# One list of TensorE instructions with short conditional blocks in place of nine arms per segment, a second buffer for the exponentials, and the next segment prepared over six steps

## Chip, cores and metric

The kernel runs on one core of one Trainium2 chip (trn2). The metric is the device time of one execution in microseconds. The kernel before ran three times: 446.67, 449.19 and 451.4 us, median 449.19.

The engines are named as in the profile: PE is TensorE (matmuls; PEld is its weight load), DVE is VectorE, ACT is ScalarE, POOL is GpSimd, SP is SyncE, which only issues DMAs. A name with a q (PEq, POOLq) is the sequencer of the engine: branches, register loads, DMA issues.

## What is computed

16384 rows of 256 features belong to 8 segments; the segment ids come unsorted. Rows are placed by id and position into padded segments, attention runs inside each segment, its result goes back to the rows, through a linear layer and a batch normalization over all rows, and is added to the input:

```python
q, k, v = feat @ Wq, feat @ Wk, feat @ Wv             # widths 32, 32, 256
starts = searchsorted(bids, arange(8))
pos = arange(N) - starts[bids]
qp, kp, vp = pad(q), pad(k), pad(v)                   # [8, 3072, .], at [bids, pos]
scores = einsum('bld,bmd->blm', qp, kp)
attn = softmax(where(mask, scores, -1e9))
rp = einsum('blm,bmd->bld', attn, vp)
t = rp[bids, pos] @ Wt
tn = (t - t.mean(0)) / sqrt(t.var(0) + 1e-5) * gamma + beta
out = feat + relu(tn)
```

Since the ids are unsorted, only few rows land inside a segment of 3072 places: with this input the segments 0 to 7 fill 4, 4, 5, 6, 6, 6, 4 and 4 tiles of 128 rows. All other rows read the first or last place of a segment.

## The kernel before

`fast_path` is written as one list of operations. The helpers of `Fast` (`mm` L790, `tr` L795, `act` L800, `copy` L805 and L806, `tt` L809, `ts` L816 and L818, `stt` L829, `recip` L842, `dma` L860, `gather` L865, `put` L875) append an operation to the list of `Program`, which works out from the memory that each one reads and writes which others it has to wait for, and hands each engine its operations in the order of writing. So the order of the work on each engine is the order in which the Python code calls the helpers. Every operation of a helper carries that helper's line in the profile, so groups are told apart by the names of tiles.

The stages:

- *Start.* The ids are loaded; DVE and small matmuls find the segment starts. For segments 0 and 1 the owned rows are counted with a scan into `lm` (L838) and `prefix`, and `make_list` turns this into a list of row numbers: two comparisons into `ge`, matmuls of `ge` with `lm`, and DVE instructions on the result (`lr`, `junk`, `jc`, `idx`); then six indirect DMAs on POOL fetch the rows into `xs`. Six places per segment are always listed and fetched, whatever its length.
- *Segments*, eight times, `e` being the current one and `n` the next. Preparing a segment: `xt_main` and `xt_rest` transpose `xs` on PE and copy it with ACT into `xT`; `project` makes q (DVE, with a copy on ACT of its last 32 partitions) and k (small DVE copies, L806) for the first four tiles (`c=0`) and the last two (`c=1`); `values` makes v times Wt (`vs`, an ACT copy); `scores(e, c, tiles)` multiplies k with q and takes the exponential on ACT into `pa` (queries of tiles 0 to 3, 512 columns per key tile) or `pb` (queries of tiles 4 and 5, 256 columns). `attend(e, u)` multiplies the exponentials with `vs` for query tile `u`; a column of ones in `vs` gives the denominators, DVE takes the reciprocal `rdens` and multiplies into `tk`, and SP stores `tk` into `t_rows` after u = 3 and u = 5.
- *Statistics.* `gather_reads` fetches how often each place is read (`reads_r`, POOL), and `moments` adds tk and its square (`sq`, ACT) times these counts into `acc` (two DVE instructions of L829 per tile).
- *Work items.* Tables over all rows (`everyone`, `tables`, `one_hot`) are cut into pieces of DVE work, and `slot()` writes one piece behind a step.
- *End.* Column sums, scale and shift; then 16 groups of 1024 rows are read (`f`), completed with a one-hot matmul and DVE additions, and stored; the places inside segments are written over by indirect DMAs of POOL (`put`), the fifth and sixth tile of a segment only where it is present (conditional block, L728).

PSUM has eight banks: 0 to 3 for scores, 4 and 5 for attends, 6 and 7 in turn (`nb()`) for all else, the lists, transposes, projections and values. `vs`, `q` and `k` have two buffers, `pa` and `pb` one.

Only the fifth and sixth tile of a segment depend on the data. On PE this is solved with arms: `region(key, arms)` opens a block for which the whole instruction list of a segment is written out for each pair of counts of `e` and `n` (three times three arms), and PE jumps into one with a register loaded from `arm` (L1055 for the loads, L770 for `e.Switch`). ACT and DVE have no arms: they do the work of six tiles in every segment. In a region the code of a step is:

```python
for u in range(FT):
    step(e, u)                  # attend(e, u), one or two moments
    if u == 0 and e + 2 < NB:
        make_list(e + 2, FT)
        gather_reads(e)
    for x in fills[u]: x()      # xt_main(n,0), xt_main(n,1), xt_rest(n), project(n,0)
    if u == 1: scores(e, 1, range(4), 0)
    if u == 2: scores(e, 1, range(4, 6), 0)
    if u == 3: project(n, 1, 1); values(n, 0, 1); scores(n, 0, range(4), None)
    if u == 4: values(n, 1, 1)
    if u == 5: values(n, 2, 1)
    slot(1)
```

The scores of `n` for key tiles 4 and 5 are made inside attend(n, 0). After segment 6 POOL gathers `ecat` from `t_rows` and loads 16 registers (`upto`, `tiles_i`, L1055) before the reads of segment 7.

## Time and profile before

One execution was profiled.

| what | us |
|---|---|
| median of three timed runs | 449.19 |
| span of the profiled execution | 481.6 |
| start, to the first attend | 43.0 |
| segments 0 to 6 | 290.1 |
| segment 7, to the last moment | 27.6 |
| statistics | 11.5 |
| 16 groups | 68.7 |
| last puts and stores | 40.7 |

The profiled execution is 32.4 us longer than the median, so its stages are read for their proportions, and a sum made in it is carried to the timed runs by the ratio 449.19/481.6. The mean clock granted to PE in it is 0.732 of full speed. An f32 matmul appears as two records.

In views by stage, a row holds the bounds, the length, and for each engine the busy time with the count of instructions in brackets; PEclk is the granted clock. In views of waits, a row names an engine, what it was about to do and what it waited for, then the total, the times and the longest. In views of groups, the numbers behind the bar are the total busy time, the mean in ns, and the idle time ahead of the group with what ended it. In the chain and the timeline a row begins with its start and its length.

### The profile page before, as it was taken

Reading aid. Unit: us, or ns where it says so; the run is one execution under the profiler, and the core shown is the slowest. Engines: PE = TensorE matmul, PEld = TensorE weight load, DVE = VectorE, ACT = ScalarE, POOL = GpSimd, SP = SyncE. Lnnn points to the kernel's source line nnn. Section 1 sums busy time; section 2 is a strip of 40 time slices with the busy share of each in tenths; the row PEclk is TensorE's granted clock in tenths of the full one; section 3 lists DMA queues with packets and bytes.
Section 4 is the critical chain, followed back from the end, with each engine's and each line's share of the span. In section 5 each row is a group of like instructions: output and inputs, shape, how many; then the busy total and the mean of one; then the engine's idle time right before and its main releaser. Section 6 shows DMA issues by size and latency. Waiting matters only on the chain.

```text
span 481.6 us, 4068 instructions
## 1 busy us (share of the span) xinstructions
PE 300.9 (62%) x1112; PEld 185.2 (38%) x1112; DVE 278.5 (58%) x775; ACT 116.4 (24%) x240; POOL 160.0 (33%) x159
## 2 busy tenths in 40 slices
PE   1368356452677486959695879797403999966000
PEld 1345233241346363747373657575301343211000
DVE  7664943322978462553554454476545999999400
ACT  0126123102142241223131323366311111100000
POOL 2340001773004522630072017700160034876350
PEclk9998857575878887788887968899855555555555
DMA  8920110120101210210011102102594599999510
GB/s 271 335 68 3 40 36 3 50 62 0 49 27 44 63 38 23 76 60 13 31 53 60 44 2 55 47 25 69 186 406 198 189 398 416 420 416 382 213 61 8
DMA packets 27218, 59.48 MB, mean 124 GB/s; under 512 B 6462, under 2 KB 19856, under 8 KB 23066
## 3 DMA queue, kind: packets, MB, share of 16 engines
q1 hardware_dynamic: 19242, 48.06, 26.7%
q0 software_dynamic: 6288, 10.01, 6.7%
q8 instruction: 35, 0.57, 0.6%
q10 hardware_dynamic: 1632, 0.66, 0.5%
q14 instruction: 21, 0.17, 0.1%
HBM read 26.42 MB, written 28.74 MB: 115 GB/s over the span
## 4 chain that ended last, share of the span: by engine, by line
PE 40%; DVE 28%; issue 12%; another core or an unknown queue 6%; DMA 3%; ACT 3%; POOL 3%; POOLq 2%; SPq 1%; DVEq 0%
PE ps L790 38%; DVE f L809 4%; DVE tk L809 3%; DVE acc L829 3%; PE ps L795 2%; DVE tk L818 2%; POOL out L875 2%; ACT pa L800 2%; DVE k L806 2%; POOLq L1055 2%; DVE junk L816 2%; DMA reads_r<-reads_of,idx 1%; DVE q L818 1%; DMA graw<-in_L_rec_gamma 1%
## 5 line engine op out<-in xcount | busy, mean ns | idle before, releaser
L865 POOL DMA_INDIRECT xs<-in_r_feat,idx x48 | 50.8, 1058 | 184.1 <-DVE junk L816 164.1
L790 PE MATMUL ps<-vs,pa 128*128 128x257 f32 x312 | 92.6, 453 | 28.4 <-DVE tk L818 16.6
L790 PEld LDWEIGHTS ps<-vs,pa 128*128 128x128 f32 x312 | 68.7, 229 | 50.4 <-issue 17.9
L842 DVE RECIPROCAL rdens<-ps 128x1 f32<-128x1 f32 x48 | 8.0, 166 | 98.8 <-PE ps L790 59.9
L790 PE MATMUL ps<-wvt,xT 128*128 128x256 f32 x156 | 46.9, 455 | 28.9 <-DVE k L806 28.9
L875 POOL DMA_INDIRECT out<-tk,idx x39 | 45.4, 1165 | 58.4 <-DVE f L809 33.7
L865 POOL DMA_INDIRECT reads_r<-reads_of,idx x48 | 48.9, 1020 | 23.8 <-issue 23.5
L790 PEld LDWEIGHTS ps<-wvt,xT 128*128 128x128 f32 x156 | 34.8, 230 | 43.9 <-DVE k L806 33.5
L800 ACT ACTIVATE xT<-ps,negx 128x512 f32<-128x512 f32 (+1 forms) x32 | 17.6, 586 | 99.5 <-PE ps L795 62.1
L790 PE MATMUL ps<-y,hot 48*128 48x256 bf16 x128 | 33.4, 409 | 12.3 <-DVE y L806 7.5
L800 ACT ACTIVATE pa<-ps,mask 128x512 f32<-128x512 f32 x48 | 29.6, 689 | 24.7 <-PE ps L790 19.3
L790 PE MATMUL ps<-f,ident 128*128 128x512 f32 x32 | 33.2, 1141 | 0.0
L790 PEld LDWEIGHTS ps<-y,hot 48*128 48x128 bf16 x128 | 12.3, 123 | 51.0 <-issue 24.1
L829 DVE SCALAR_TENSOR_TENSOR acc<-tk,reads_r,acc 128x256 f32<-128x256 f32 x48 | 22.9, 477 | 15.0 <-DMA reads_r<-reads_of,idx 14.6
L809 DVE TENSOR_TENSOR tk<-tk,ss 128x768 f32<-128x768 f32 x32 | 30.5, 955 | 0.6
L809 DVE TENSOR_TENSOR f<-f,ps 128x512 f32<-128x512 f32 x48 | 30.0, 680 | 0.8 <-PE ps L790 0.8
L805 ACT COPY f<-ps 128x512 f32<-128x512 f32 x16 | 9.4, 586 | 66.1 <-PE ps L790 66.1
L829 DVE SCALAR_TENSOR_TENSOR acc<-sq,reads_r,acc 128x256 f32<-128x256 f32 x48 | 23.0, 479 | 3.1 <-ACT sq L800 3.1
L818 DVE TENSOR_SCALAR tk<-ps,rdens 128x256 f32<-128x256 f32 x48 | 23.2, 484 | 1.8
L800 ACT ACTIVATE sq<-tk 128x256 f32<-128x256 f32 x48 | 20.2, 425 | 15.3 <-DVE acc L829 13.5
L790 PE MATMUL ps<-q,k 32*128 32x512 f32 (+2 forms) x124 | 23.1, 654 | 0.0
L795 PE MATMUL ps<-ident,xs 128*128 128x128 f32 x78 | 15.5, 336 | 11.7 <-DVE lr L809 6.8
(229 smaller groups left out, 367.3 us busy)
## 6 DMA issues: line engine op xcount, KB each, us to landing
f<-in_r_feat SPq DMA_DIRECT2D x16, 1024.0 KB, 17.1
out<-f SPq DMA_DIRECT2D x16, 1024.0 KB, 4.8
xs<-zt SPq DMA_DIRECT2D x8, 768.0 KB, 9.9
t_rows<-tk SPq DMA_DIRECT2D x8, 512.0 KB, 3.0
t_rows<-tk SPq DMA_DIRECT2D x8, 256.0 KB, 2.7
eb<-edge_of SPq DMA_DIRECT2D x16, 96.0 KB, 4.5
xs<-in_r_feat,idx POOLq DMA_INDIRECT x48
reads_r<-reads_of,idx POOLq DMA_INDIRECT x48
```

The source lines that it names most:

```text
L790: "PE", lambda e: e.matmul(out, lhsT, rhs, start=start, stop=stop, skip_group_check=True),
L795: return self.op("PE", lambda e: e.transpose(out, in_, ident), [in_, ident], [out], pred=pred)
L800: "ACT", lambda e: e.activation(out, in_, func, bias=bias, scale=scale), [in_, *more], [out]
L805: return self.op("ACT", lambda e: e.copy(out, in_), [in_], [out])
L806: return self.op(eng, lambda e: e.tensor_copy(out, in_), [in_], [out])
L809: return self.op(eng, lambda e: e.tensor_tensor(out, a, b, op), [a, b], [out])
L816: lambda e: e.tensor_scalar(out, a, s1, s2, op0, op1, accum_out=accum)
L818: else e.tensor_scalar(out, a, s1, s2, op0, op1),
L829: else e.scalar_tensor_tensor(out, a, s, b, op0, op1),
L865: lambda e: e.indirect_dma_start(out=out, out_offset=None, in_=table, in_offset=bass.IndirectOffsetOnAxis(ap=ind, axis=0), bounds_check=n ...
L875: lambda e: e.indirect_dma_start(out=table, out_offset=bass.IndirectOffsetOnAxis(ap=ind, axis=0), in_=src, in_offset=None, bounds_check=n ...
L1055: regs[key] = e.value_load(ap, min_val=lo, max_val=hi)
```

## The change

- *PE in one list.* `region`, `arms` and `e.Switch` are gone. An operation written under `with pg.given(e, k)` is done only when the register of segment `e` (0, 1 or 2 for four, five or six tiles) is greater than k; runs of operations with the same condition form one `e.If` block (now at L764). PE has 22 such blocks per segment; ACT has seven and DVE one, which there skip the work of missing tiles. A conditional operation signals nothing itself: whoever waits for it waits for the next unconditional operation on its engine. The three engines load the register once per segment (L686).
- *`pa` has two buffers*, and the scores of `n` for key tiles 4 and 5 are made in segment `e` as well. `pb` keeps one; its exponentials are written as eleven instructions of 128 or 256 columns in place of six of 256.
- *tk and q on ACT.* The multiplication of the attend's result with `rdens` moves from DVE to ACT; q is written by two ACT instructions from PSUM.
- *The next segment over six steps* (diff below). The lists' comparisons (`list_tests`) are made in u = 5 of the segment before the one that uses them, the list halves use score banks 2 and 3. Those of segment 2 are made ahead of the loop.
- *Moments and reads.* The reads of segment e are gathered in segment e + 1; no moments in segments 0 and 1, one or two per step afterwards.
- *Group loads.* All eight buffers of the final stage lie over `pa[0]` and what follows it; the loads of groups 0 to 5 are issued inside segment 7 (groups 0 to 3 in u = 0), those of 6 and 7 after it. Before, all eight came after it.

```diff
-                    if len(arms) == 1:
-                        one(arms[0])
-                    else:
-                        for a in e.Switch(reg["reg"](e), len(arms)):
-                            one(arms[a])
+                    with e.If(self.regs[(eng, o.when[0])] > o.when[1]):
+                        for x in ops[k:end]:
+                            emit(e, x)
...
-    pa = new("pa", [P, FT, QA])
-    pb = new("pb", [P, FT, QB])
+    pa[0] = new("pa0", [P, FT, QA])
...
+    pa[1] = new("pa1", [P, FT, QA])
...
+    def present(e, t):
+        return ExitStack() if t < 4 else pg.given(e, t - 4)
...
-        pg.ts(qe[0:96, lo : lo + n], b[0:96, 0:n], cqk[0:96, :], ALU.add)
-        pg.copy("ACT", qe[96:P, lo : lo + n], qe[0:32, lo : lo + n])
-        for t in range(n // P):
-            g = 32 * t
-            pg.copy("DVE", ke[g : g + 32, c, :], b[96:P, t * P : (t + 1) * P])
+        with present(e, 4 * c):
+            pg.act(qe[0:96, lo : lo + n], b[0:96, 0:n], AF.Identity, bias=cqk[0:96, :])
+            pg.act(qe[96:P, lo : lo + n], b[0:32, 0:n], AF.Identity, bias=cqk[0:32, :])
+            for t in range(n // P):
+                g = 32 * t
+                pg.copy("DVE", ke[g : g + 32, c, :], b[96:P, t * P : (t + 1) * P])
...
-        pg.ts(tk[:, m, :], po[:, 0:D], rdens[:, m : m + 1], ALU.mult)
+        pg.act(tk[:, m, :], po[:, 0:D], AF.Identity, scale=rdens[:, m : m + 1])
...
+            if ahead <= NB and u == 0:
+                first = list_half(ahead, 0, ps_s[2])
+            attend(e, u)
...
+            if ahead <= NB and u == 0:
+                first()
+                if LTs == FT:
+                    second = list_half(ahead, 1, ps_s[3])
+            if e >= 2:
+                for _ in range(2 if u % 2 or len(lag) > 12 else 1):
+                    if lag and lag[0][0] < (e if u > 1 else e - 1):
+                        moments(*lag.pop(0))
+            if e >= 1 or u >= 1:
+                slot(2 if e == 0 else 1)
+            attended(e, u)
...
             if u == 1:
-                scores(e, 1, range(4), 0)
...
+                gather_reads(e - 1) if e else None
+            if n < NB:
+                if u == 0:
+                    xt_main(n, 0)
+                    xt_main(n, 1)
+                if u == 1:
+                    xt_rest(n)
+                if u == 2:
+                    scores(e, 1, None)
+                    project(n, 0)
+                if u == 3:
+                    project(n, 1)
+                    scores(n, 0, range(4))
+                if u == 4:
+                    values(n, 0)
+                    scores(n, 0, range(4, 6))
+                if u == 5:
+                    values(n, 2)
+                    values(n, 1)
+                    if e + 3 <= NB:
+                        list_tests(e + 3, FT if e + 3 < NB else LT)
+            else:
...
+                if u == 1:
+                    gather_reads(e)
+                if u == 0:
+                    for g in range(4):
+                        group_in(g)
```

How the instructions move, at three places. In the rows, psN is the PSUM bank, `ge` and `lm` belong to the lists, `w4` to the projection, `wvt` to the values; "waits at_X" is a semaphore of engine X.

PE, in segment 1, arm of six and six tiles, from the projection of segment 2 to its values, before:

```order
L790 MATMUL ps6<-xT_55,w4_78 128x512 x2
L790 MATMUL ps7<-xT_55,w4_78 128x256 [waits at_ACT]
L790 MATMUL ps7<-xT_55,w4_78 128x256
L790 MATMUL ps6<-wvt_79,xT_55 128x256 [waits at_DVE]
L790 MATMUL ps6<-wvt_79,xT_55 128x256 x3
L790 MATMUL ps0<-q0_56,k0_57 128x512
L790 MATMUL ps1<-q0_56,k0_57 128x512
L790 MATMUL ps2<-q0_56,k0_57 128x512
L790 MATMUL ps3<-q0_56,k0_57 128x512 [waits at_ACT]
L790 MATMUL ps4<-vs1_58,pb_53 128x257 x6
```

and now, in segment 0, whose steps are the same:

```order
L799 MATMUL ps7<-xT_54,w4_79 128x512
L799 MATMUL ps5<-vs0_53,pa0_52 128x257 [waits at_ACT]
L799 MATMUL ps5<-vs0_53,pa0_52 128x257 x2
L764 COMPARE_AND_BRANCH
L799 MATMUL ps5<-vs0_53,pa0_52 128x257
L764 UNCONDITIONAL_BRANCH
...
L799 MATMUL ps0<-q1_63,k1_64 128x512 [waits at_ACT,at_DVE]
L799 MATMUL ps1<-q1_63,k1_64 128x512 [waits at_DVE]
L799 MATMUL ps2<-q1_63,k1_64 128x512 [waits at_DVE]
L799 MATMUL ps3<-q1_63,k1_64 128x512 [waits at_ACT,at_DVE]
...
L799 MATMUL ps7<-wvt_80,xT_54 128x256 x4
```

An attend stands between the projection and the scores; the values, which waited for DVE straight after the projection, come behind the scores and wait for nothing.

PE, at the start of segment 1, the arm of six and six tiles before:

```order
L770 BRANCH_PREFETCH_HINT
L790 MATMUL ps4<-vs1_58,pa_52 128x257
L790 MATMUL ps0<-q1_59,k1_60 128x512
L790 MATMUL ps1<-q1_59,k1_60 128x512
L790 MATMUL ps4<-vs1_58,pa_52 128x257 x2
L790 MATMUL ps4<-vs1_58,pa_52 128x257 [waits at_ACT] x2
L790 MATMUL ps4<-vs1_58,pa_52 128x257
L790 MATMUL ps7<-lm_61,ge_62 128x131 [waits at_DVE] x2
```

and now:

```order
L686 TENSOR_LOAD tiles_i_128
L686 ISA x2
L799 MATMUL ps2<-lm_57,ge_58 128x131 [waits at_DVE] x2
L799 MATMUL ps2<-lm_57,ge_58 128x131 x4
L799 MATMUL ps4<-vs1_66,pa1_65 128x257 x2
L799 MATMUL ps4<-vs1_66,pa1_65 128x257 [waits at_ACT]
L764 COMPARE_AND_BRANCH
L799 MATMUL ps4<-vs1_66,pa1_65 128x257
```

The first list half now stands ahead of the attend, in a score bank, and the scores of key tiles 4 and 5 are no longer inside the attend.

POOL, around the end of segment 6, before:

```order
L865 DMA reads_r<-reads_of,idx 128x1 x12
L865 DMA ecat<-t_rows,eidx 128x256
L1055 TENSOR_LOAD upto
L1055 ISA x2
L1055 TENSOR_LOAD tiles_i
```

and now:

```order
L874 DMA reads_r<-reads_of,idx 128x1 x6
L874 DMA ecat<-t_rows,eidx 128x256
L686 TENSOR_LOAD upto
...
L686 ISA x2
L874 DMA reads_r<-reads_of,idx 128x1 x12
L874 DMA tl<-t_rows,ridl 128x256 x3
```

Six gathers of reads moved from ahead of the `ecat` gather to behind the register loads.

607 lines of the change are left out of this document (286 added, 321 removed).

## Prediction

> **What bounds the kernel now.** I read the busy slices of the page first, then a table by stage, then what TensorE (PE) waits for in the stages that the change touches.
>
> ```profile
> PE 300.9 (62%) x1112; PEld 185.2 (38%) x1112; DVE 278.5 (58%) x775; ACT 116.4 (24%) x240; POOL 160.0 (33%) x159
> ...
> PE 40%; DVE 28%; issue 12%; another core or an unknown queue 6%; DMA 3%; ACT 3%; POOL 3%; POOLq 2%; SPq 1%; DVEq 0%
> ```
>
> No engine is full: PE, the busiest, is busy for 62% of the span, and it leads the chain that ended last with 40%. The shares are means over unlike stages, so the next table cuts the span at the start of each segment's first attend.
>
> ```profile
> core 0: us, PE busy (x) PEld busy (x) DVE busy (x) ACT busy (x) POOL busy (x), PEclk, DMA share, GB/s
> ...
> 43.01:84.15 41.14, 22.45 (x84) 13.69 (x82) 25.01 (x91) 13.57 (x28) 1.14 (x2) 0.74 0.07 24
> 84.15:137.42 53.27, 24.81 (x90) 17.91 (x91) 26.55 (x74) 12.38 (x27) 22.93 (x23) 0.69 0.13 37
> 137.42:181.69 44.27, 32.27 (x137) 22.52 (x137) 29.28 (x100) 12.83 (x27) 16.92 (x16) 0.81 0.16 48
> 181.69:230.49 48.80, 38.91 (x153) 27.42 (x153) 21.56 (x62) 13.10 (x27) 14.62 (x14) 0.79 0.16 48
> 230.49:276.12 45.63, 34.82 (x152) 25.47 (x153) 21.60 (x62) 13.09 (x27) 12.51 (x12) 0.85 0.13 41
> 276.12:315.41 39.29, 33.31 (x137) 23.47 (x137) 18.46 (x61) 12.22 (x26) 19.54 (x18) 0.83 0.12 33
> 315.41:333.06 17.65, 14.71 (x69) 10.63 (x68) 11.24 (x31) 11.64 (x26) 0.00 (x0) 1.00 0.14 47
> 333.06:360.68 27.62, 8.93 (x40) 7.47 (x41) 15.63 (x42) 9.25 (x23) 10.08 (x10) 0.73 0.69 262
> 360.68:372.22 11.54, 4.08 (x5) 1.00 (x5) 6.66 (x21) 2.00 (x3) 0.00 (x0) 0.50 0.55 222
> 372.22:440.92 68.70, 63.85 (x159) 20.20 (x160) 66.75 (x87) 8.79 (x15) 35.21 (x29) 0.50 0.90 364
> ...
> ```
>
> The loop over segments 0 to 6 is the stretch 43.01 to 333.06: 290.05 us, of which PE is busy 22.45 + 24.81 + 32.27 + 38.91 + 34.82 + 33.31 + 14.71 = 201.3 and idle 88.8. DVE (153.7) and ACT (88.8) are well below that, so in the loop PE's own work and its gaps set the pace, but for segments 0 and 1, where DVE is busier than PE. The clock matters as well: multiplying each row's busy time by its PEclk gives 162.6 us of work at full clock, so 38.7 of the 201.3 are the lower clock. The last 148.5 us, where DVE (66.75 of 68.70), the puts and the last DMAs set the end, are the same code in both kernels from the statistics on.
>
> PE's gaps in the loop, by what it waited for:
>
> ```profile
> PE ps L790 <- DVE k L806: 28.9, 7, 6.3
> ...
> PE ps L790 <- DVE tk L818: 16.6, 3, 14.2
> PE ps L790 <- issue: 14.8, 5, 6.2
> ...
> PE ps L790 <- DVE ge L818: 7.6, 4, 1.9
> PE ps L795 <- DVE lr L809: 6.8, 5, 1.5
> ```
>
> Columns: total, times, longest. These five are 74.7 of the 88.8 us.
>
> **Part by part.** *The wait for k (28.9).* `values(n,0)` runs straight after the projection and needs a PSUM bank that DVE still reads for q and k; the scores behind it on PE stand too. The new list puts attend(e,3) between `project(n,0)` and `scores(n,0)`, and attend(e,4) ahead of `values(n,0)`. The cover is real PE work:
>
> ```profile
> 333.06 7.20 PE L790 MATMUL ps<-vs,pa 128*128 128x257 f32 x32 [0.86 <-ACT sq L800]
> 323.25 1.88 PE L790 MATMUL ps<-xT,w 128*128 128x512 f32 x4
> L818 DVE TENSOR_SCALAR q<-ps,cqk 96x512 f32<-96x512 f32 x7 | 5.2, 742 | 7.1 <-PE ps L790 6.4 <-remote 0.7
> L806 DVE COPY k<-ps 32x128 f32<-32x128 f32 x44 | 12.9, 294 | 0.9
> L800 ACT ACTIVATE pa<-ps,mask 128x512 f32<-128x512 f32 x44 | 27.1, 688 | 24.3 <-PE ps L790 18.8 <-issue 5.4
> L800 ACT ACTIVATE pb<-ps,mask 128x256 f32<-128x256 f32 x42 | 17.4, 480 | 7.0 <-PE ps L790 3.9 <-remote 3.1
> L818 DVE TENSOR_SCALAR tk<-ps,rdens 128x256 f32<-128x256 f32 x41 | 19.8, 484 | 1.5
> ```
>
> A record of an attend takes 7.20/32 = 0.225 us, so an attend of a six-tile segment (12 records) covers 2.7 us. Four k copies are 1.18; q moves to ACT as two acts of at most the 688 ns of a 512-wide one. All 28.9 is taken off. What comes back: on ACT q now stands behind the second exponentials, ten of 128 columns and one of 256. From 688 and 480 ns a 128-wide act is an estimated 376, so these are 4.2 us where six of 480 were 2.9; with q (1.4) and a tk (0.42) ACT needs 6.0 us. PE's work between is project(n,0) (1.88), the attend (2.7) and project(n,1) (about 1): 5.6. I charge 1.1 for each of three six-tile segments, 3.4 in all (bounds 0 and the 28.9 itself, if the wait only changes its name).
>
> *The wait for tk (16.6)* is mostly one stall, 14.2 long, seen on the chain too:
>
> ```profile
> 102.48 14.36 another core or an unknown queue
> 112.80 1.00 POOL L865 DMA_INDIRECT reads_r<-reads_of,idx  x1 [0.30 <-issue]
> 206.92 4.61 another core or an unknown queue
> L865 POOL DMA_INDIRECT reads_r<-reads_of,idx x42 | 42.9, 1021 | 12.8 <-issue 12.5 <-DVE lr L809 0.3
> ```
>
> It lies in a run of 24 gathers on POOL that ends at 113.8; in later segments the run is 12 long and the stall 4.61. The new order never queues 24 at once, so I take 16.6 off and put one such 4.6 back. If these stalls came from somewhere else, the 16.6 stays (bounds 0 and 16.6).
>
> *The list waits (7.6 + 6.8).* The comparisons for the list of e+2 are made in the last step of the segment before, and its halves have PSUM banks of their own. The cover is the rest of that segment's DVE queue, 0.4 us each; without it the 14.4 comes back.
>
> *Dispatch (14.8).* Each segment's jump into one of nine arms goes:
>
> ```profile
> L770 PEldq COMPARE_BRANCH  x18: 288/399/5012, 40.4 to 341.0; - x18
> L728 POOLq COMPARE_BRANCH  x16: 34/45/53, 393.8 to 457.0; - x16
> L1055 PEldq TENSOR_LOAD <-arm x9: 296/304/738, 22.7 to 78.9; - x9
> ```
>
> Minimum, median and maximum in ns: the jumps cost up to 5012. In their place PE evaluates 22 conditions per segment and 2 at the end, 178 in all; with segments of 4, 4, 5, 6, 6, 6, 4 and 4 tiles, 101 of them skip. The nearest rows are POOL's short conditional blocks, built the same way, at 45 ns, and PE's own shortest jump at 288. I take 0.1 us, nearer the form than the engine: 17.8 us of sequencer time, of which 44 conditions lie in segments 0 and 1 and 22 in segment 7, where DVE or POOL sets the pace; 112 are left, and I expose 10. Bounds: 178 x 0.034 = 6 all hidden, so 0, and 178 x 0.399 = 71. The loads of the registers, 0.30 us each on three engines per segment, lie beside waits. [...]
>
> *Clock.* The row at 315 shows PE with 14.71 of 17.65 busy at 1.00; the rows with longer gaps show 0.69 to 0.85. With two thirds of the idle time gone the loop is like that row more often. Bounds: 0 and all of the 38.7; I take 18, about half. [...]
>
> *tk to ACT.* 41 x 484 ns leaves DVE (19.8 us) and comes to ACT, which was busy 88.8 of 290; both beside PE.
>
> *Start.* The owners and tests of segment 2 are made before the loop, and the first list half stands ahead of attend(0,0) on PE: some 20 small DVE instructions, 5 us by the 0.29 of a k copy, partly under the projections: +3 (bounds 0 and 6).
>
> *Tail.* The reads of a segment are gathered one segment later, so behind the ecat gather and 16 register loads POOL has twelve, not six:
>
> ```profile
> 337.71 0.30 POOLq L1055
> ...
> 346.25 0.28 POOLq L1055
> ...
> 352.76 5.53 DMA reads_r<-reads_of,idx
> ...
> 360.15 0.49 DVE acc L829
> 360.68 4.09 PE ps L790 x4
> ```
>
> The last reads, at 358.3, release the last moments and these the statistics at 360.68. Six more gathers at (42.9 + 12.8)/42 = 1.33 us are +8.0, and nothing covers them: DVE has only the moments to do (bounds 4, should the register loads start earlier against the segment's end, and 8).
>
> *Group loads.* Four of the final stage's loads are issued in segment 7, on SP ahead of its stores of t rows. Before, all landed before their use at 372.22, so nothing is gained; a late store would cost at most its own
>
> ```profile
> 334.17 2.19 DMA t_rows<-tk
> ```
>
> and I take 0.
>
> **The sum.** -74.7 + 3.4 + 4.6 + 10 - 18 + 3 + 8 = -63.7 us against the profiled span of 481.6: 417.9. The three timed runs have a median of 449.19, 0.933 of that span; by this ratio 417.9 is **390 us**.
>
> **Rivals.** *The wait moves to ACT.* ACT takes its list in order; tk now waits there for a reciprocal that stands behind moments and list work on DVE, and the exponentials, q and xT wait behind tk. If the k wait of 28.9 comes back as a wait for q, the gain is 34.8: 446.8, timed 417. For it: the 6.0 against 5.6 above. Against it: ACT is busy only 13 us in segments of 44 to 49.
>
> *Slower: a hop costs PE what a jump does.* Place: the 101 skipped blocks, 90 of which belong to the segments of four tiles. My sum without the 10 for branches is 73.7; it is eaten when a skip costs 73.7/101 = 0.73 us. The median PE jump is 0.40 and the longest 5.0; at 1.0 the end is 481.6 - 73.7 + 101 = 508.9, timed 475. Against it: POOL's 45 ns.
>
> *Slower: the granted clock stays at a half once PE is dense*, as the row 372.22 to 440.92 shows (63.85 of 68.70 busy at 0.50). Then the 162.6 of work take 325; with start, tail and their 11 us 527.7, timed 492. It decides below a mean of 0.64 (162.6 over the 253 us that are left). Against it: 1.00 in the dense row at 315.41.
>
> *The gaps only move*: attends wait for tk, lists for POOL, and segments 0 and 1 stay with DVE; within 1% of 449.
>
> **How the numbers follow.** Forecast 0.65; wait on ACT 0.22; no change 0.04; dear hops 0.06; half clock 0.03. A measurement of this kernel tells about 1% from no change (446.67 to 451.4). Faster is 0.65 + 0.22 = 0.87, same 0.04, slower 0.09. The range: if every wait goes, hops are free and the clock is full, 481.6 - 74.7 - 38.7 + 11 = 379, timed 354; the ACT rival with 13 us more of branches or waits reaches 430. So 355 to 430.
>
> **What would show it.** Right: in the loop no wait of PE for k over 1 us, no branch record over 1 us, PEclk above 0.85 from segment 2 on, the loop's seven segments in about 218 us, and 35 us instead of 27.62 from the end of segment 6's attends to the last moment. Wrong: waits of PE on q, pa or tk of ACT that sum to over 20 us; branch records of PE with a median above 0.4 us; a clock of 0.5 to 0.7 in rows where PE is busy over 85%; or a loop above 250 us.

## The result and the profile after

The changed kernel takes 424.81 us (median of four runs, 423.68 to 429.4), the kernel before 449.63 (median of four, one of them taken beside it); the ratio is 0.948, 95% interval 0.941 to 0.954. Here and below medians are over all executions and ratios over those within 1.5% of their kernel's fastest, so that a ratio can differ a little from the quotient of two medians, and a single execution of the kernel before at 861 us, beside e1 to e4, is in none. So it is faster by 5%, by 24.8 us where 59 were forecast, and 424.81 lies inside the range of 355 to 430. The profiled execution spans 422.2 us; the forecast of that span was 417.9. The span of before in its profile was 481.6. **The difference of the spans came as forecast, the difference of the times did not.**

The page of the kernel after, busy time by engine:

```profile
PE 287.8 (68%) x1162; PEld 181.8 (43%) x1162; DVE 246.3 (58%) x715; ACT 122.7 (29%) x266; POOL 162.0 (38%) x159
```

The table by stage of the kernel after, cut at each segment's first attend (segments 0 to 6, then segment 7 to the statistics; columns as in the prediction):

```profile
47.81:73.00 25.19, 19.05 (x86) 13.63 (x83) 20.08 (x76) 8.31 (x16) 6.78 (x6) 0.80 0.15 47
73.00:96.95 23.95, 20.59 (x95) 14.35 (x93) 21.54 (x57) 11.34 (x23) 14.00 (x12) 0.93 0.24 73
96.95:130.94 33.99, 27.57 (x139) 20.20 (x137) 22.16 (x78) 16.50 (x38) 12.90 (x12) 0.94 0.18 55
130.94:171.21 40.27, 34.82 (x168) 26.27 (x167) 20.05 (x60) 17.59 (x44) 12.54 (x12) 0.88 0.19 53
171.21:211.73 40.52, 35.47 (x170) 26.48 (x167) 17.71 (x54) 17.01 (x41) 12.14 (x12) 0.87 0.15 45
211.73:243.05 31.32, 29.17 (x146) 22.64 (x143) 13.18 (x52) 13.74 (x34) 12.24 (x12) 0.89 0.14 42
243.05:267.12 24.07, 17.61 (x71) 12.57 (x69) 8.70 (x33) 10.10 (x22) 12.14 (x12) 0.86 0.14 43
267.12:300.93 33.81, 12.11 (x46) 9.17 (x44) 10.98 (x31) 7.75 (x20) 16.47 (x16) 0.65 0.77 289
```

The loop takes 219.3 us (the terms of the sum give 215.4, and about 218 was announced), PE is busy for 184.3 of it and idle for 35.0; the first attend starts at 47.81 in place of 43.01 (forecast +3), and segment 7 to the statistics takes 33.8 us (forecast 35.6). What PE still waits for in the loop (of the rows of PE the five longest):

```profile
PE ps L799 <- ACT q L809: 11.5, 4, 5.2
PE ps L799 <- DVE ge L827: 9.3, 3, 3.1
PE ps L799 <- DVE lm L847: 5.0, 1, 5.0
PE ps L799 <- ACT vs L814: 3.6, 4, 1.2
PE ps L799 <- ACT pa L809: 2.1, 1, 2.1
```

The waits for k, tk and the jumps are gone from this list, and that for `ge`, the comparisons of the lists, is still there. New are those for q, `lm` (which belongs to the lists as well) and pa, and that for vs has grown; three of these four carry the name of ACT. In segment 6, PE's weight loads still wait 5.6 us for k, beside the longest wait for q (see e17).

### The profile page after: what moved, and what is told of

Read it like the earlier page. It is cut to its first block, busy times and chain, and to the rows that moved or that the text cites. A ratio compares the mean times of both kernels' runs of the same rounds, so it can differ in the third digit from the quotient of the medians.

```text
span 422.2 us, 4412 instructions
## 1 busy us (share of the span) xinstructions
PE 287.8 (68%) x1162; PEld 181.8 (43%) x1162; DVE 246.3 (58%) x715; ACT 122.7 (29%) x266; POOL 162.0 (38%) x159
## 5 line engine op out<-in xcount | busy, mean ns | idle before, releaser
L799 PE MATMUL ps<-vs,pa 128*128 128x257 f32 x312 | 80.2, 410 | 0.0
L799 PEld LDWEIGHTS ps<-vs,pa 128*128 128x128 f32 x312 | 62.7, 206 | 13.2 <-issue 3.3
L809 ACT ACTIVATE tk<-ps,rdens 128x256 f32<-128x256 f32 x48 | 22.8, 475 | 128.1 <-DVE rdens L851 128.1
L838 DVE SCALAR_TENSOR_TENSOR acc<-sq,reads_r,acc 128x256 f32<-128x256 f32 x48 | 23.1, 481 | 48.4 <-ACT sq L809 48.4
L799 PE MATMUL ps<-wvt,xT 128*128 128x256 f32 x156 | 41.3, 413 | 5.2 <-ACT vs L814 3.6
L799 PEld LDWEIGHTS ps<-wvt,xT 128*128 128x128 f32 x156 | 31.4, 207 | 18.9 <-ACT vs L814 6.0
L799 PE MATMUL ps<-q,k 32*128 32x512 f32 (+2 forms) x154 | 25.1, 563 | 13.8 <-ACT q L809 11.5
L809 ACT ACTIVATE pa<-ps,mask 128x512 f32<-128x512 f32 x39 | 23.9, 689 | 12.9 <-PE ps L799 12.8
L799 PE MATMUL ps<-vs,pb 128*128 128x257 f32 x82 | 25.7, 477 | 0.0
L799 PEld LDWEIGHTS ps<-vs,pb 128*128 128x128 f32 x82 | 19.3, 242 | 9.7 <-issue 5.3
L799 PE MATMUL ps<-xT,w 128*128 128x512 f32 (+1 forms) x60 | 21.0, 483 | 0.3 <-ACT tk L809 0.3
L799 PE MATMUL ps<-lm,ge 128*128 128x131 bf16 x102 | 11.4, 253 | 13.6 <-DVE ge L827 13.1
```

The source lines that it names most:

```text
L799: "PE", lambda e: e.matmul(out, lhsT, rhs, start=start, stop=stop, skip_group_check=True),
L809: "ACT", lambda e: e.activation(out, in_, func, bias=bias, scale=scale), [in_, *more], [out]
L838: else e.scalar_tensor_tensor(out, a, s, b, op0, op1),
```

## The experiments

Experiments 1 to 4 ran on one chip, 5 to 8 on a second, 9 to 12 on a third, 13 to 16 on a fourth, 17 and 18 on a fifth. Each is compared with the kernel before on its own chip, and that turned out to matter: before takes 448 to 449 us on the first and fifth, 478 to 481 on the other three. Below, the former are called chips without stalls, the latter chips with stalls. Medians in us:

| experiment | kernel | before there | this | ratio to before (95%) |
|---|---|---|---|---|
| e1 | before, unchanged | 449.2 | 449.8 | |
| e2 | before, values behind the scores | 449.2 | 442.7 | 0.987 (0.979 to 0.994) |
| e3 | after, reads and registers early | 449.2 | 395.2 | 0.880 (0.876 to 0.885) |
| e4 | after, twice the blocks on PE | 449.2 | 426.3 | 0.942 (0.935 to 0.949) |
| e5 | after, one buffer pa | 477.8 | 438.1 | 0.914 (0.905 to 0.923) |
| e6 | after, tk on DVE | 477.8 | 423.7 | 0.886 (0.874 to 0.899) |
| e7 | before, reads and registers early | 477.8 | 472.6 | 0.985 (0.973 to 0.998) |
| e8 | after, four edits | 477.8 | 418.8 | 0.872 (0.862 to 0.882) |
| e9 | after, unchanged | 481.1 | 437.8 | 0.916 (0.904 to 0.927) |
| e10 | e5 again | 481.1 | 437.8 | 0.905 (0.893 to 0.918) |
| e11 | e8 again | 481.1 | 419.6 | 0.875 (0.864 to 0.886) |
| e12 | e8 with gathers apart | 481.1 | 394.7 | 0.827 (0.816 to 0.837) |
| e13 | before, gathers apart | 478.4 | 450.4 | 0.942 (0.938 to 0.947) |
| e14 | after, gathers apart | 478.4 | 433.5 | 0.906 (0.901 to 0.912) |
| e15 | e12 again | 478.4 | 395.1 | 0.826 (0.820 to 0.832) |
| e16 | e12, values earlier | 478.4 | 384.3 | 0.804 (0.798 to 0.811) |
| e17 | e6 again | 448.0 | 416.1 | 0.930 (0.925 to 0.934) |
| e18 | e16, tk on DVE | 448.0 | 371.0 | 0.827 (0.823 to 0.831) |

### Was the profiled execution of before like its timed ones?

**e1, before unchanged.** The theory was that the 481.6 us held stalls which the timed executions do not hold; the rival that the profiler always slows the kernel with arms.

> The kernel before, unchanged. Theory 1 (the profiled execution of before held about 30 us of stalls that its timed executions do not hold, so scaling a sum made in it was the error): spans of the new executions lie at 444 to 450, 2 to 3 us below their times, not at 481; the loop over segments 0 to 6 takes 255 to 265 us in place of 290; the pieces of unknown queue on the chain sum to under 8 us in place of 28.9. Rival (the profiler always slows the kernel with arms): the new profile again spans 470 to 490 while the times stay at 449.

The new profile spans 449.0 us, and the ten executions of this run, the profiled one among them, span 439.8 to 449.6, each some 1.8 us below its time: the profiler does not by itself stretch this kernel to 481. By stage (segments 0 to 6, then segment 7 to the statistics) and by PE's waits in the loop:

```profile
44.45:85.33 40.88, 22.61 (x84) 13.88 (x82) 24.62 (x91) 13.56 (x28) 0.99 (x1) 0.75 0.07 24
85.33:123.72 38.39, 24.05 (x90) 17.13 (x91) 26.43 (x74) 12.38 (x27) 24.49 (x23) 0.74 0.18 51
123.72:162.25 38.53, 30.76 (x137) 21.89 (x137) 29.93 (x100) 12.72 (x27) 17.24 (x16) 0.82 0.19 55
162.25:202.90 40.65, 34.95 (x153) 25.55 (x153) 21.66 (x62) 12.76 (x27) 14.89 (x14) 0.87 0.20 57
202.90:243.72 40.82, 34.91 (x152) 25.62 (x153) 21.66 (x62) 12.76 (x27) 13.10 (x12) 0.87 0.17 46
243.72:281.24 37.52, 31.86 (x136) 22.76 (x137) 18.70 (x62) 12.25 (x27) 19.29 (x18) 0.86 0.12 35
281.24:300.98 19.74, 16.42 (x68) 11.62 (x69) 11.53 (x32) 12.03 (x27) 0.00 (x0) 0.91 0.13 42
300.98:328.48 27.50, 8.92 (x40) 7.47 (x41) 15.26 (x42) 8.88 (x23) 9.97 (x10) 0.73 0.69 256
```

```profile
PE ps L790 <- DVE ge L818: 15.6, 5, 6.8
PE ps L790 <- DVE k L806: 14.9, 7, 4.9
...
PE ps L790 <- issue: 8.0, 4, 3.3
PE ps L795 <- DVE lr L809: 6.4, 5, 1.5
...
PE ps L790 <- DVE tk L818: 2.3, 2, 1.6
```

The loop takes 256.5 us in place of 290.05; outside it little differs (the start 44.45 against 43.01, segment 7 27.50 against 27.62). The whole surplus of the first profile lay in the loop. On the chain the pieces of unknown queue, 28.9 us before, are none. Segment 1, which held the stall of 14.36, is 38.39 us in place of 53.27, with the same 24 gathers in a row. PE is idle for 61.0 us, not 88.8; the wait for k is half, that for tk almost nothing, that for the comparisons of the lists (`ge`) twice as long.

**e9, after unchanged, on a chip where before takes 481.** By then the chips had shown themselves; theory 2 was that semaphores of PE come late on some chips while POOL runs a long row of gathers.

> The changed kernel, unchanged, beside the others of this call on one chip. Theory 2 (chips differ: on some, semaphores of PE reach DVE late while POOL runs a long row of gathers; the kernel before takes 478 there and 449 elsewhere): where before takes 475 to 483, this takes 436 to 444, ratio 0.91 to 0.93, with four or five stalls of 4 to 6 us in its profile; where before takes 446 to 451, this takes 422 to 429, ratio 0.947, and no such stall. Rival (the changed kernel is the same everywhere): 422 to 429 on both, ratio 0.88 where before takes 478.

437.8, a gain of 43 us there against 25 elsewhere. Its profile (span 431.6) has a stall again, on the chain and in the waits:

```profile
111.62 6.27 another core or an unknown queue
```

```profile
ACT pb L809 <- remote: 6.6, 2, 5.8
DVE k L815 <- remote: 6.4, 1, 6.4
```

So the changed kernel has these stalls too, on such a chip, and the rival (the same time everywhere) falls. They are fewer than expected: two pieces on the chain, 7.5 us in all, in place of four or five of 4 to 6.

**e13, before with its gathers apart**, where before takes 478. The arms and the order of all other engines stay:

```diff
-    gather_reads(0)
+    gather_reads(0, range(3))
...
                 make_list(e + 2, FT)
-                gather_reads(e)
-            elif u == 0 and e < NB:
+            elif u == 0 and last:
                 gather_reads(e)
+            if not last and u in (2, 3, 4):
+                i = u - 2 if e == 1 else {2: 1, 4: 2}.get(u)
+                if i is not None:
+                    gather_reads(0 if i == 0 else e, range(3, 6) if i in (0, 2) else range(3),
+                                 [rdens[:, e * FT + u : e * FT + u + 1]])
```

The last argument makes the gathers wait for the reciprocal of that attend; in `make_list` nothing changes.

> The kernel before, arms and order unchanged; only the gathers of reads are issued three at a time, each three behind the reciprocal of an attend, so that the rows of 24 and 18 gathers become rows of 6 to 15 and those of 12 become rows of 6. Theory (the stalls in long rows are the whole of the 30 us): where before takes 475 to 483, this takes 450 to 460; where before takes 449, this stays within 1% of it. Rival (such a chip is slower in other ways too, or the stalls follow the number of gathers): 470 or more there.

450.4 us, on a chip where the unchanged kernel needs 478.4. Segment 7 starts where it does in e1, at 300.98 there and here at

```profile
300.77 7.20 PE L790 MATMUL ps<-vs,pa 128*128 128x257 f32 x32 [1.05 <-ACT sq L800]
```

No piece of unknown queue is left on the chain. So the stalls in long rows of gathers account, but for 1.2 us, for the 29 us between the chips for the kernel before, and by their size and place for those between the profile of before and its times. Nothing else about such a chip shows as slower. This kernel was not run on a chip without stalls, so it is not shown that splitting the rows gains nothing by itself.

### What the parts of the change do

**e2, before, with the order of values alone.** `project(n,0)` one step earlier, `values(n,0)` behind the scores:

```diff
-                0: [first[0]], 1: [first[1]], 2: [first[2]], 3: [lambda: project(n, 0, 1)],
+                0: [first[0]], 1: [first[1]], 2: [first[2], lambda: project(n, 0, 1)], 3: [],
...
                 project(n, 1, 1)
-                values(n, 0, 1)
                 scores(n, 0, range(4), None)
             if u == 4 and not last:
+                values(n, 0, 1)
                 values(n, 1, 1)
...
```

> The kernel before with its arms, one part of the change alone: project(n,0) one step earlier, so that attend(e,3) lies between it and the scores, and values(n,0) behind the scores. Theory 1 with the k wait real: PE's wait for k (28.9 us in the old profile) falls below 8 and the time falls by 12 to 25 us, to 425 to 437. Rival (the k wait is an effect of the same stalls, or the gap only moves to q): under 5 us, 444 to 450.

442.7, 6.5 us faster, between theory and rival. PE's wait for k fell from 14.9 to 3.9 us, 11 us; about four of them came back as waits for a reciprocal (one of 3.9 us in e1, three with 8.1 here):

```profile
PE ps L790 <- DVE rdens L842: 8.1, 3, 4.0
...
PE ps L790 <- DVE k L806: 3.9, 2, 2.1
```

**e4, after, a block for each conditional matmul**: 362 branch records on PE in place of 178.

```diff
-                    while end < len(ops) and ops[end].when == o.when:
+                    while end < len(ops) and ops[end].when == o.when and (eng != "PE" or end == k):
```

> The changed kernel, where each conditional matmul has a block of its own on PE: about 184 more branches than the 178. At the 0.2 us median of the PE branch records they are 37 us of sequencer time. Theory (they hide under the queue of matmuls, but for the segments with few tiles): 0 to 6 us slower, 425 to 431. Rival (each branch is exposed): 37 us slower, about 460.

426.3 against 424.8 of the changed kernel (before at 449.2 and 449.6): 1.5 us, inside the intervals. The records of the kernel after on PE and POOL (minimum, median, maximum in ns):

```profile
L764 PEldq COMPARE_BRANCH  x178: 65/202/422, 34.5 to 288.1; - x178
...
L764 POOLq COMPARE_BRANCH  x16: 34/45/53, 334.0 to 397.9; - x16
```

A condition costs PE's sequencer 202 ns, twice my price, and hides: in e4 segment 7 starts 3.3 us later (270.44 against 267.12) for 184 more, 18 ns each if all of it is theirs; the executions of e4 scatter by more than that (422.2 to 433.7).

**e5 and e10, one buffer for the first exponentials:**

```diff
     pa[0] = new("pa0", [P, FT, QA])
+    lap = addr(pa[0])
...
     pa[1] = new("pa1", [P, FT, QA])
+    pa[0] = pa[1]
...
+    fb = [at(f"f{i}", [P, GT, D], F32, lap + 8192 * i) for i in range(8)]
...
```

The buffers of the final stage (`fb`) stay where they were.

> The changed kernel with one buffer for the exponentials of tiles 0 to 3 in all segments. Theory (in the new order the scores of the next segment stand behind attend(e,3), the last reader of that buffer, so the second one is never needed): no change, 422 to 428. Rival (the exponentials of the next segment run while the attends still read): 10 us or more slower.

> One buffer for the first exponentials, beside the changed kernel on one chip. Theory (the second buffer is never needed in the new order): within 1% of the run of the changed kernel in this call. Rival: 10 us or more slower than it.

e5 gave 438.1 with nothing of the changed kernel beside it; it could not be read by itself, since its chip is one on which before takes 478. e10 stood beside e9: 437.82 against 437.81. The second buffer is worth nothing that these runs can tell (each interval is about 1.2% to either side). It only leaves room for the early group loads, which lie over the first one.

**e6 and e17, tk on DVE again:**

```diff
-        pg.act(tk[:, m, :], po[:, 0:D], AF.Identity, scale=rdens[:, m : m + 1])
+        pg.ts(tk[:, m, :], po[:, 0:D], rdens[:, m : m + 1], ALU.mult)
```

> The changed kernel with tk multiplied on DVE again (48 x 0.48 us back to DVE, off ACT). Theory (the 11.5 us that PE waits for q come from DVE waiting for late reads and from the second exponentials ahead of q on ACT, not from tk on ACT): within 4 us of the changed kernel, 421 to 429. Rival 1 (tk waiting on ACT for a reciprocal holds up q): 6 to 12 us faster, 413 to 419. Rival 2 (DVE, busy 21.5 of 24 us in segment 1, was the place to relieve): 6 us or more slower.

> The changed kernel with tk on DVE. Theory (tk on ACT waits there for a reciprocal and holds q and the exponentials behind it): ratio to before 0.875 to 0.895 where before takes 475 to 483, and 0.92 to 0.94 (413 to 422) where it takes 446 to 451. Rival (the earlier chip was simply milder): 0.905 to 0.925 on a chip with stalls, 0.94 to 0.955 on one without.

Ratios 0.886 and 0.930, against 0.916 and 0.948 of the changed kernel on chips of the same kind; in us 8.7 faster where before takes 448 to 450 (416.1 against 424.8, on two chips), 14.4 faster than e5 on one chip with stalls, and e5 is by e10 as fast as the changed kernel. My theory for e6 (nothing) fell, its first rival stands: in this order, moving tk to ACT is a loss. The profile of the kernel after shows how, in segment 3. First DVE, then ACT, then PE:

```profile
144.76 0.48 DVE L838 SCALAR_TENSOR_TENSOR acc<-tk,reads_r,acc 128x256 f32<-128x256 f32 x1 [4.72 <-DMA reads_r<-reads_of,idx]
...
146.64 0.11 DVE L851 RECIPROCAL rdens<-ps 128x1 f32<-128x1 f32 x1
```

```profile
146.78 0.47 ACT L809 ACTIVATE tk<-ps,rdens 128x256 f32<-128x256 f32 x1 [5.20 <-DVE rdens L851]
147.15 3.05 ACT L809 ACTIVATE pb<-ps,mask 128x128 f32<-128x128 f32 x11
150.01 1.43 ACT L809 ACTIVATE q<-ps,cqk 96x512 f32<-96x512 f32 x2
```

```profile
150.88 2.74 PE L799 MATMUL ps<-q,k 32*128 32x512 f32 x8 [2.24 <-ACT q L809]
```

DVE stands 4.72 us for reads that POOL has yet to fetch; behind them stands the reciprocal, behind that tk on ACT (5.20 idle), behind tk the second exponentials and q, and behind q PE. In e17 the same place has no such wait on ACT, the exponentials follow PE at once:

```profile
147.74 3.06 ACT L809 ACTIVATE pb<-ps,mask 128x128 f32<-128x128 f32 x11 [3.26 <-PE ps L799]
150.61 1.43 ACT L809 ACTIVATE q<-ps,cqk 96x512 f32<-96x512 f32 x2
```

and PE's waits for q, 11.5 us in the kernel after, come to 0.3. Segments 3 to 5 take 99.8 us in place of 112.1. Of these 12.4 us the waits for q were 6.2 (2.2, 1.8 and 2.2); PE's busy time falls by 7.4 as well, at a granted clock of 0.92 to 0.95 in place of 0.87 to 0.89, and the waits for `ge` are 1.0 longer. Against this, segments 0 and 1, where DVE is the busiest engine, take 4.5 us more (53.6 for 49.1).

The longest wait for q, 5.2 us in segment 6, was not tk's doing. First the kernel after, then e17, at the same place:

```profile
258.04 2.74 PE L799 MATMUL ps<-q,k 32*128 32x512 f32 x8 [5.22 <-ACT q L809]
```

```profile
248.57 3.05 PE L799 MATMUL ps<-q,k 32*128 32x512 f32 x8 [4.91 <-DVE k L815]
```

In both, DVE stands there for reads, 8.03 and 7.54 us, and has the reciprocal and k behind them in its list. With tk on DVE, q is early and PE waits for k.

**e3, after, reads and registers early:**

```diff
+    reads_in = {1: [0], 2: [1], 3: [2, 3], 4: [4], 5: [5, 6], 6: [7]}
...
-                gather_reads(e - 1) if e else None
+                for r in reads_in.get(e, ()):
+                    gather_reads(r)
...
-                if u == 1:
-                    gather_reads(e)
...
+        if e == 3:
+            for e_ in range(NB):
+                pg.register("POOL", ("g", e_), upto[0:1, e_ : e_ + 1], NG, 1)
+                pg.register("POOL", e_, tiles_i[0:1, e_ : e_ + 1], 2)
...
```

The register loads behind segment 6 go.

> The changed kernel, with the reads of segments 0 to 7 gathered in segments 1, 2, 3, 3, 4, 5, 5 and 6 and POOL's 16 register loads in segment 3. Theory (the last reads are what the statistics wait for, and the late reads hold DVE and through it q in segment 6): the stretch from segment 7's first attend to the statistics falls from 33.8 to about 17 us and the 5.2 us wait for q goes, so 18 to 22 us faster than the changed kernel, 403 to 407. Rival (the reads were waited for beside moments that had to be done anyway): 8 us or less, 417 to 424.

395.2, 29.6 us below the changed kernel, more than the 18 to 22 expected. First the kernel after, then e3, at the statistics:

```profile
300.93 2.08 PE L799 MATMUL ps<-acc,ones 128*128 128x512 f32 x2 [9.07 <-DVE acc L838]
```

```profile
251.53 7.29 PE L799 MATMUL ps<-vs,pa 128*128 128x257 f32 x32
...
268.67 2.08 PE L799 MATMUL ps<-acc,ones 128*128 128x512 f32 x2 [6.40 <-DVE acc L838]
```

The last stretch is 17.1 us in place of 33.8, as expected; and the loop ends 15.6 us earlier (251.53 against 267.12), 1.6 of them from a start in which the two kernels do the same. The two edits were not tried apart. DVE's wait for reads in the loop, first the kernel after, then e3:

```profile
DVE acc L838 <- DMA reads_r<-reads_of,idx: 23.1, 4, 8.0
```

```profile
DVE acc L838 <- DMA reads_r<-reads_of,idx: 4.8, 1, 4.8
...
PE ps L799 <- ACT q L809: 2.6, 2, 2.3
```

With the reads early PE waits 2.6 us for q in place of 11.5, and tk is still on ACT. So most of these waits needed both, tk on ACT and late reads in DVE's list; what tk on ACT costs with early reads is open.

**e7, the same edit in the kernel before** (reads of segment 7 right behind those of segment 6; registers in segment 3):

```diff
-            elif u == 0 and e < NB:
+            elif u == 0 and e == NB - 2:
                 gather_reads(e)
+                gather_reads(e + 1)
...
+        if e == 3:
+            for e_ in range(NB):
+                load("POOL", ("g", e_), upto[0:1, e_ : e_ + 1], NG, 1)
+                load("POOL", ("t", e_), tiles_i[0:1, e_ : e_ + 1], 2)
...
```

> The kernel before with its arms and its order, only POOL changed: the reads of segment 7 gathered right behind those of segment 6, the 16 register loads in segment 3. Theory (the statistics wait for POOL's chain in the old kernel as well): the 27.5 us from segment 7's first attend to the statistics fall to 14 to 17, so 11 to 14 us faster than before, 435 to 439. Rival (the chain was hidden behind moments that have to be done): under 5 us.

Only 5.2 us, and not to be read as the rival: this chip stalls, the edit makes another row of 24 gathers, in segment 6 (278.9 to 311.2), and a stall of 10.44 us lies on the chain at 296.61. The part that the theory was about came true: from segment 7's first attend (333.29) to the statistics (349.58) it is 16.3 us, where 14 to 17 were expected. What the edit gives in time without the stall was not tried.

### Stalls and the length of the rows

**e8 and e11, after with four edits** (e3, and: list comparisons in u = 3, `scores(e, 1)` in u = 1, moments of segments 6 and 7 sooner).

```diff
                 if u == 1:
                     xt_rest(n)
+                    scores(e, 1, None)
                 if u == 2:
-                    scores(e, 1, None)
                     project(n, 0)
...
+                    if e + 3 <= NB:
+                        list_tests(e + 3, FT if e + 3 < NB else LT)
...
-                    if lag and lag[0][0] < (e if u > 1 else e - 1):
+                    if lag and (lag[0][0] < (e if u > 1 else e - 1) or (e >= NB - 2 and len(lag) > 2)):
...
```

> The changed kernel with four edits: early reads and register loads as in the third experiment; the list comparisons in u = 3 in place of u = 5; the second scores one step earlier, so that q no longer stands behind their exponentials on ACT; moments of segments 6 and 7 two steps behind their attend. Theory (each removes a wait seen in the trace: 9.3 us for the comparisons, 11.5 for q, 6.4 for the last moments): 8 to 14 us below the third experiment's 395, 381 to 387. Rival (the waits only change their names, since DVE and ACT set the pace): 392 to 396.

> The four edits, beside the changed kernel on one chip. On a chip without stalls 381 to 390 (395 of the third experiment less the waits for the comparisons, q and the last moments); on a chip with them 416 to 420 as before, with stalls of up to 13 us in the rows of 15 and 18 gathers. Rival (the edits gave nothing and the third experiment's chip was merely the better one): 392 to 396 where before takes 449.

418.8 and 419.6, both where before takes 478 to 481; the 381 to 387 of e8 were wrong for such a chip, and e11's second case came in. It has rows of 15 and 18 gathers, as e3 has, where no stall shows, and one stall in the longer shows what such a stall is. First POOL's first gather and last, then PE, then ACT ("remote" is a signal whose sender the view can't name):

```profile
219.03 1.09 POOL L874 DMA_INDIRECT xs<-in_r_feat,idx  x1 [18.51 <-DVE idx L838]
...
241.30 1.00 POOL L874 DMA_INDIRECT reads_r<-reads_of,idx  x1 [0.30 <-issue]
```

```profile
223.89 1.25 PE L799 MATMUL ps<-q,k 32*128 32x128 f32 x22
...
234.20 0.91 PE L799 MATMUL ps<-vs,pa 128*128 128x257 f32 x3 [1.03 <-issue]
236.32 0.38 PE L799 MATMUL ps<-vs,pa 128*128 128x257 f32 x1 [1.21 <-issue]
```

```profile
240.62 3.05 ACT L809 ACTIVATE pb<-ps,mask 128x128 f32<-128x128 f32 x11 [15.04 <-remote]
```

PE has the second scores done at 225.1. ACT starts their exponentials at 240.62, 15 us later, when POOL's row is about to end, and the trace puts that idle time down to a signal from elsewhere; PE meanwhile gets out one to four records at a time, with up to 1.2 us of idle "issue" between them.

The trace's record of semaphores tells whose delay it is. ACT has done the two branches ahead of these exponentials by 225.3, so it is not short of instructions. The semaphore that it waits for is the one that PE raises, and this shows no update between 224.88 and 240.60, although records of PE that raise it end at 225.77, 227.94, 230.32 and 236.70. The four updates come at 240.60 and from 244.93 to 245.12, while PE does nothing. So PE's signal is late, not ACT. The same can be counted in every trace of the changed kernel and its variants: an update more than 0.5 us behind the latest record of PE that could have raised it. There is none in the kernel after, e3, e4, e17 and e18; there are 4 to 26 in each of e5, e6, e8 to e12 and e14 to e16, all of them while POOL issues an indirect DMA or within 5 us after one.

**e12 and e15, gathers apart**: each three gathers of reads wait for the reciprocal of an attend.

```diff
+    reads_in = {1: [0, 1], 2: [2], 3: [3], 4: [4, 5], 5: [6], 6: [7]}
...
+            halves = [(r, h) for r in reads_in.get(e, ()) for h in range(2)]
+            at_u = {2: 0, 4: 1} if len(halves) == 2 else {2: 0, 3: 1, 4: 2, 5: 3}
+            if halves and u in at_u:
+                r, h = halves[at_u[u]]
+                gather_reads(r, h, rdens[:, e * FT + u : e * FT + u + 1])
...
```

The reads of segments 1, 2 and 5 also come one segment earlier than in e11.

> The four edits, with the gathers of reads issued three at a time, each three behind the reciprocal of an attend, so that no row of gathers on POOL is longer than six to nine. Theory 2: on a chip with stalls 15 to 30 us faster than the kernel with four edits, 390 to 403, and stalls of unknown queue below 6 us in all; on a chip without them within 3 us of it. Rival (the stalls come with the number of gathers, not the length of their rows): no change on either chip.

> The kernel with four edits and gathers apart, unchanged. On a chip with stalls 393 to 399 again; on a chip without them (before at 449) 386 to 394, since nothing is left there for the stalls to cost.

394.7 and 395.1, 25 us below e11, with the same number of gathers. On the chain the unknown queue is 5.8 us in e12 (3.5 in e15), 21.7 in e11. Two rows of 12 are left in e12. What the three edits besides e3's are worth is not shown: 394.7 on a chip with stalls stands against e3's 395.2 on one without.

**e14, after with gathers apart and nothing else:**

```diff
-                gather_reads(e - 1) if e else None
+                gather_reads(e - 1, range(3), [rdens[:, e * FT + u : e * FT + u + 1]]) if e else None
+            if u == 3 and e:
+                gather_reads(e - 1, range(3, 6), [rdens[:, e * FT + u : e * FT + u + 1]])
...
```

> The changed kernel, only the gathers of the reads of segments 0 to 6 split into threes behind the reciprocals of u = 1 and u = 3. Theory: on a chip with stalls 424 to 430 in place of 438, on a chip without them 422 to 429. Rival: 435 or more on a chip with stalls.

433.5, between theory and rival. The unknown queue on the chain is down to 1.4 us; but the second half of the reads now comes later, and DVE waits longer for it in the loop than the 23.1 us above (23.2 in e9):

```profile
DVE acc L838 <- DMA reads_r<-reads_of,idx: 38.6, 8, 8.1
```

**e16 and e18, on from e12.** `values(n,1)` moves from u = 5 to u = 4, a small matmul and a small ACT copy close the step; e18 also puts tk on DVE, as in e6.

```diff
                     scores(n, 0, range(4, 6))
+                    values(n, 1)
                 if u == 5:
                     values(n, 2)
-                    values(n, 1)
+                    mark(ps_s[2])
+                    pg.copy("ACT", spot[:], ones[:, 0:1])
```

> As the kernel before this one, with values(n,1) made in u = 4 in place of u = 5 (a small matmul and a small ACT copy then close the step). Theory (PE waits 3 us for the last values' copy on ACT at the start of segments 3, 4 and 5, and 4.9 us in front of segment 7): 5 to 10 us faster than the kernel with gathers apart in this call. Rival (the wait moves to the exponentials on ACT in front of those copies): within 3 us of it.

> The kernel of the sixteenth experiment (384.3) with tk on DVE. Theory: 3 to 10 us faster, 374 to 381. Rival 1 (there the waits for q are gone already, and tk on DVE only stands in front of the list work): within 3 us of 384. Rival 2 (DVE sets the pace there): 388 or more.

384.3, 10.8 us below e15 beside it; the wait for the values was in e12

```profile
PE ps L799 <- ACT vs L814: 15.7, 7, 4.9
```

and is 2.8 in e16. e18 takes 371.0, the fastest here: 0.827 of the kernel before on a chip where that takes 448. Since e16 was not run there, how much of its 13 us below e16 is tk and how much the chip stays open.

## Why the prediction was wrong

**The step that failed is the last of the sum**, "by this ratio 417.9 is 390 us". It took the 32 us by which the profile of before exceeds its times for a stretch of all stages alike, and scaled the changed kernel with it. The runs showed stalls of one stage, the loop, in their place: another profile of the same kernel has none and spans 449.0 (e1), and such stalls go with the chip and with long rows of gathers (e9, e13). Which chip the first profile ran on is not on record. The changed kernel's span and its times agree (422.2 and 424.8), as those of before do in e1 (449.0 and 449.8), so there was nothing to scale.

Without the ratio the forecast would have been 418, 1.6% off, and that would have been luck in part. The 63.7 us were taken off an execution with stalls: of the 74.7 us of waits in the sum, e1 has 47.2. The rest went because the profile of the kernel after holds no stalls, not by the change. Against e1 the change is worth 26.8 us of span; on a chip with stalls it gains 43 us of time (e9).

So each term of the sum is set against e1, the kernel before without stalls:

- *k, 28.9 off and 3.4 back*: e1 has 14.9 of it. The order does take most of it away (11 in e2), but what came back is 11.5 us of waits for q, not 3.4. That was my rival with 0.22, and for 6.3 of the 11.5 its mechanism is the right one (q behind tk and the exponentials on ACT, tk behind DVE). The other 5.2, in segment 6, are DVE's wait for reads, which made k as late as q (e17). My argument against the rival, ACT busy for 13 of 44 us, counted the engine's work and not its list. So did the 3.4, from 6.0 us on ACT against 5.6 on PE: ACT needs 3.05 + 1.43 + 0.47 = 4.95 there and starts late.
- *tk, 16.6 off and one 4.6 back*: 2.3 in e1; the rest was the stall. On a chip with stalls the changed kernel stalls as well (e9).
- *Lists, 14.4 off*: 22.0 in e1 (15.6 + 6.4). 9.3 remain for `ge`, since the comparisons stand at the end of DVE's list in u = 5, where I had said that the rest of the queue covers them, and 5.0 for `lm` are new: 14.3 in all.
- *Dispatch, 14.8 off and 10 back*: 8.0 in e1, 0.3 left, and about 178 x 18 ns = 3 for the branches, if they cost what the added ones do (e4). The 0.1 us a condition leaned on POOL's 45 ns: in the kernel after, the median record is 202 ns on PE, against 45 on POOL and ACT.
- *Clock, 18 off*: work at full clock, summed as before, is 162.9 us after and 163.1 in e1; the busy times of 184.3 and 195.6 are 21.4 and 32.5 above it. 11 gained, 17 against the first profile, whose 38.7 did not go as a whole.
- *tk to ACT, nothing*: a loss of 8.7 us (e17), as long as the reads are late (e3).
- *Start, +3*: 47.81 against 44.45, 3.4. *Tail, +8*: 33.8 against 27.5, 6.3. But late reads cost far more than the tail: DVE waits 23.1 us for them in the loop too, which I had not priced, and moving them back with the registers gave 29.6 (e3).
- *Second buffer*: rightly without a term (e10).

So in spans on a chip without stalls: loop -37.2 (idle 61.0 to 35.0, busy 195.6 to 184.3), start +3.4, tail +6.3, the rest +0.7: 449.0 to 422.2.

Two figures of the rivals do not follow from the terms. If the whole k wait comes back as a wait for q, the 3.4 is no longer due beside it, and the gain is 38.2, not 34.8. The 253 us of the half clock are 247 by the same sum, so that rival would decide below 0.66.

The signs that I had named would not have caught the error: no wait for k in PE's list, 219 us of loop, 34 us of tail were all as announced. One sign was in the first profile, quoted and not used: 6% of the chain (28.9 us) in pieces that belong to no known queue, in an execution 32.4 us longer than the median.

Open: what differs between the chips, and why rows of gathers hold up PE's signals on some. Only the length and the place of the rows were varied.

## What to carry to other kernels

Where a profile is several per cent longer than the times, profile the unchanged kernel again, as e1 did, and find the stage with the surplus; if it is one stage with pieces that no queue explains, take those pieces out of the sum and do not scale. When a small operation moves to an idle engine, look at what stands behind it in that engine's list and what it will wait for: tk cost 0.48 us on DVE; on ACT it waited 5 us for DVE's late reads, and the exponentials and q waited with it. And a transfer that nothing waits for in one place may be late in every other place once its consumer's list holds more important work (DVE stood 23.1 us for the reads in the loop): move such transfers as early as their inputs allow (29.6 us in e3, the register loads with them), and on a chip with such stalls in short rows (28 us in e13).

## What the runs showed of the hardware

- On the chips of e5 to e16, signals of PE came late while POOL issued rows of indirect DMAs: 4 to 26 updates more than 0.5 us late in each trace of the changed kernel and its variants there. In e11 ACT got one 15 us late in a row of 18, and PE's own issue slowed to one to four records at a time. The first profile has such a stall, 14.36 us on its chain, in a row of 24. With most rows split into three to nine, 0 to 5.8 us were left on the chain (e12 to e16).
- On the two other chips no such stall is on the chain, with the same row of 24 (e1), with rows of 15 and 18 (e3) and with rows of 12 (e17). No trace of the changed kernel or a variant there shows an update of PE's semaphore over 0.5 us late.
- A conditional block costs PE's sequencer 65 to 422 ns (median 202), ACT's and POOL's 45 (median), and 184 more of them on PE moved the end by 1.5 us, which is within the scatter (e4).
